# Prompt-type pooling rewritten as one recurrence per chunk, with its weights computed on 32 segments

## Chip, cores and metric

The kernel runs on one core of one Trainium2 chip. The metric is the device time of one execution in microseconds (us): the median of three runs of the kernel before is 1771.83 us (1770.89 to 1772.97). Engines are named as the profile names them: PE is TensorE (matmul), PEld its weight load, DVE is VectorE, ACT is ScalarE, POOL is GpSimd, SP is SyncE. POOL, SP and ACT also issue DMAs[...].

## What is computed

Sixteen images `x` of 512 positions by 512 features, all in fp32.

```python
# stage 1: a two-layer MLP whose last 128 outputs come from one of 16 experts, chosen per image
h = gelu(x @ fc1_w.T + fc1_b)                       # 512 -> 2048
shared = h @ fc2_w.T + fc2_b                        # 2048 -> 384
expert = h @ experts_w[idx].T + experts_b[idx]      # 2048 -> 128
x1 = x + concat(shared, expert)
# stage 2: attention pooling with one score per position; the mask depends on the prompt type
scores = tanh(x1 @ W1 + b1) @ v                     # one number per position l
mask = prefix (l <= j) if type 0, postfix (l >= j) if type 1, l != j if type 2
p = softmax(where(mask, scores[l], -1e30))          # over l, for each j
out = x1 + (p @ x1) / count(mask)
```

Since the score does not depend on j, row j of `p @ x1` is a running sum: a prefix of exponentials times x1 for type 0, a suffix for type 1, the whole without one element for type 2. A recurrence along the positions, rescaled whenever the running maximum grows, computes it.

## The kernel before, in words

Features lie on the partitions (four chunks of 128), positions along the free axis, so `x1T` of one image is 128 x 4 x 512. The program is written out by hand (`manual_schedule`, line 60): what each engine does, and in which order, is the order of the code. The image loop stands at line 493; image b's MLP is interleaved with the pooling of image b-1.

**fc1** (`fc1_group`, line 240) works in four groups of 256 + 256 hidden rows. Each group is a two-by-two block product done with seven block products instead of eight, in the order ba, bb, bc, bd, ba, bc, bd, named by the PSUM bank they write. The operands are sums of blocks: those of the weights are computed once, for image 0, on DVE (`sums`, line 69; four 128x512 sums per group), written to DRAM and read back for later images (`fetch`, line 85); those of x are four sums on DVE (`x_sums`, line 115). Between the products DVE joins results: u2 (line 260), u3 (264), c22 (268), c21 (276), c12 (281); ACT copies bank ba once (256) and applies gelu (250). A bank is written again once its readers are through: the second product into bc waits for u3, the second into bd for c22, the first product of the next group, into ba, for the gelu of ba. In group 1 of each image (group 2 of image 0) DVE also makes four 128x1024 sums of the expert's weights (`lower`, line 172), one in each of four slots.

**fc2** (`fc2`, line 285) is the same scheme with 16 matmuls to a half product. Its operand sums are four 128x2048 DVE instructions (313 to 321). The residual x arrives by DMA again (`residual`).

**Pooling of the image before** is a generator whose steps are handed out by `slot()` after each fc1 product (line 507) and by `at()` between the fc2 products (line 520). `scores` (347) makes the projection `pa`, tanh, and a score product whose stationary operand is v copied to 128 columns, so that every partition holds the whole score row. `recur` (362) then works on 128 partitions x 512 positions for all prompt types at once: a forward and a backward running maximum (scans), their exponentials on ACT (three passes, each between two table loads), three weights e for the part before, the own position and the part behind, the denominators, one reciprocal. Then for each of the four chunks nine DVE instructions (439 to 455): two products, a forward and a backward scan, three products and two sums. `flip` (459) transposes a finished chunk back on PE, ACT copies it to SBUF, POOL writes it to DRAM. In the image loop (line 523) 37 steps of the recurrence are spread over fc2. After the last image the whole pooling of image 15 stands alone (542 to 546).

**The start.** The x blocks of image 0 are loaded over ACT's queue and the first weights over SP's. Seven small inputs (idx, prompt types, biases, w1, v) go over POOL's queue behind the four stores of the first weight sums (139 to 151). DVE's order there is: x sums, four weight sums, `rows` from idx (159), the copy of v (186), masks and counts (193 to 212), then the sums of group 1 and u2. `load_fc2` puts two transfers of 2 MB and 1 MB on SP's queue ahead of the weights of group 2.

Of the kernel before, what the change touches and what calls it, by code (L numbers as in the profile page):

```python
# [17 lines left out]
def tile_cond_experts_then_prompt_pool(  # L18
# [26 lines left out]


# [38 lines left out]
    def fetch(b, g):  # L85
# [11 lines left out]
        for n, t in (("a11", w["a11"]), ("a21", a21), ("a22", w["a22"]), ("a12", w["a12"])):  # L97
            nc.sync.dma_start(t, part_of(n))
# [26 lines left out]
    x_next = load_x(0, nc.scalar)  # L125
    fc1b_sb = const.tile([P, NH], F32, name="fc1b_sb")
    nc.scalar.dma_start(fc1b_sb, fc1_b)
    xs_next = x_sums(0, x_next)
    w_next = fetch(0, 0)
    work(4)  # L130
    fc2_sb = const.tile([P, NH, 2 * P], F32, name="fc2_sb")
# [5 lines left out]

    idx_sb = const.tile([P, B], I32, name="idx_sb")
    nc.gpsimd.dma_start(idx_sb, idx.partition_broadcast(P))
    pt_sb = const.tile([P, B], I32, name="pt_sb")  # L140
    nc.gpsimd.dma_start(pt_sb, ptype.partition_broadcast(P))
    fc2b_sb = const.tile([P, NS], F32, name="fc2b_sb")
    nc.gpsimd.dma_start(fc2b_sb, fc2_b)
    expb_sb = const.tile([E, PART], F32, name="expb_sb")
    nc.gpsimd.dma_start(expb_sb, exp_b)
    w1_sb = const.tile([P, ND, A], F32, name="w1_sb")
    nc.gpsimd.dma_start(w1_sb, w1)
    b1_sb = const.tile([A, 1], F32, name="b1_sb")
    nc.gpsimd.dma_start(b1_sb, b1)
    v_sb = const.tile([A, 1], F32, name="v_sb")  # L150
    nc.gpsimd.dma_start(v_sb, v)
# [7 lines left out]
    nc.vector.tensor_scalar(rows, idx_sb, float(P), part_f, ALU.mult, ALU.add)  # L159

# [17 lines left out]
    ex_next = load_expert(0)  # L178

# [5 lines left out]
    v_bc = const.tile([A, P], F32, name="v_bc")  # L185
    nc.vector.tensor_copy(v_bc, v_sb.to_broadcast([A, P]))


    cnt_i = p1.tile([P, 2, S], I32, tag="ff", name="cnt_i")
    nc.gpsimd.iota(cnt_i[:, 0, :], pattern=[[1, S]], base=1, channel_multiplier=0)  # L190
    nc.gpsimd.iota(cnt_i[:, 1, :], pattern=[[-1, S]], base=S, channel_multiplier=0)
    cnts = const.tile([P, 2, S], F32, name="cnts")
    nc.vector.tensor_copy(cnts, cnt_i)


    is0 = const.tile([P, B], F32, name="is0")
    nc.vector.tensor_scalar(is0, pt_sb, 0.0, None, ALU.is_equal)
    is1 = const.tile([P, B], F32, name="is1")
    nc.vector.tensor_scalar(is1, pt_sb, 1.0, None, ALU.is_equal)
    is2 = const.tile([P, B], F32, name="is2")  # L200
    nc.vector.tensor_scalar(is2, pt_sb, 2.0, None, ALU.is_equal)

    pen = const.tile([P, 3, B], F32, name="pen")
    for i, sel in enumerate((is1, is2, is0)):
        nc.vector.tensor_scalar(pen[:, i, :], sel, NEG, None, ALU.mult)

    cnt2 = const.tile([P, B], F32, name="cnt2")
    nc.vector.tensor_scalar(cnt2, is2, float(S - 1), None, ALU.mult)
# [138 lines left out]
    def scores(b, x1T):  # L347
        pa = ps_l.tile([A, S], F32, tag="l", name=f"pa_{b}")
        for dc in range(ND):
            nc.tensor.matmul(  # L350
                pa, w1_sb[:, dc, :], x1T[:, dc, :], start=(dc == 0), stop=(dc == ND - 1)
            )
        aT = p1.tile([A, S], F32, tag="aT", name=f"aT_{b}")
        nc.scalar.activation(aT, pa, AF.Tanh, bias=b1_sb)
        yield
        psc = ps_l.tile([P, S], F32, tag="l", name=f"psc_{b}")
        nc.tensor.matmul(psc, v_bc, aT, start=True, stop=True)
        sc = p1.tile([P, S], F32, tag="sc", name=f"sc_{b}")
        nc.scalar.copy(sc, psc)
        yield sc  # L360

    def recur(b, x1T, sc, ready):
        V = nc.vector

        def rev(t):
            return t[..., S - 1 :: -1]

        def border(tag, name, at, value):
            t = p1.tile([P, S + 1], F32, tag=tag, name=f"{name}_{b}")
            nc.gpsimd.memset(t[:, at : at + 1], value)  # L370
            return t

        mf, mb = border("mf", "mf", 0, NEG), border("mb", "mb", S, NEG)
        V.tensor_tensor_scan(mf[:, 1:], sc, sc, NEG, ALU.max, ALU.max)
        yield
        ff = p1.tile([P, 2, S], F32, tag="ff", name=f"ff_{b}")
        V.tensor_tensor(ff[:, 0, :], mf[:, :S], mf[:, 1:], ALU.subtract)
        yield  # L380
        V.tensor_tensor(ff[:, 1, :], sc, mf[:, 1:], ALU.subtract)
        yield
        V.tensor_tensor_scan(rev(mb), rev(sc), rev(sc), NEG, ALU.max, ALU.max)
        nc.scalar.activation(ff, ff, AF.Exp)
        yield
        fb = p1.tile([P, 2, S], F32, tag="fb", name=f"fb_{b}")
        V.tensor_tensor(fb[:, 0, :], mb[:, 1:], mb[:, :S], ALU.subtract)
        yield
        V.tensor_tensor(fb[:, 1, :], sc, mb[:, :S], ALU.subtract)
        yield  # L390

        t = p1.tile([P, S], F32, tag="t", name=f"t_{b}")
        mx = p1.tile([P, S], F32, tag="mx", name=f"mx_{b}")
        V.tensor_scalar(t, mf[:, :S], pen[:, 0, b : b + 1], None, ALU.add)
        nc.scalar.activation(fb, fb, AF.Exp)
        yield
        V.scalar_tensor_tensor(mx, sc, pen[:, 1, b : b + 1], t, ALU.add, ALU.max)
        yield
        V.scalar_tensor_tensor(mx, mb[:, 1:], pen[:, 2, b : b + 1], mx, ALU.add, ALU.max)
        yield  # L400
        e = p1.tile([P, 3, S], F32, tag="e", name=f"e_{b}")
        for i, src in enumerate((mf[:, :S], sc, mb[:, 1:])):
            V.scalar_tensor_tensor(e[:, i, :], src, pen[:, i, b : b + 1], mx, ALU.add, ALU.subtract)
            yield
        zf, zb = border("mf", "zf", 0, 0.0), border("mb", "zb", S, 0.0)
        V.tensor_tensor_scan(zf[:, 1:], ff[:, 0, :], ff[:, 1, :], 0.0, ALU.mult, ALU.add)
        nc.scalar.activation(e, e, AF.Exp)
        yield
        V.tensor_tensor_scan(rev(zb), rev(fb[:, 0, :]), rev(fb[:, 1, :]), 0.0, ALU.mult, ALU.add)
        yield  # L410
        cnt = p1.tile([P, S], F32, tag="mx", name=f"cnt_{b}")
        V.tensor_scalar(cnt, cnts[:, 0, :], is0[:, b : b + 1], cnt2[:, b : b + 1], ALU.mult, ALU.add)
        yield
        V.scalar_tensor_tensor(cnt, cnts[:, 1, :], is1[:, b : b + 1], cnt, ALU.mult, ALU.add)
        yield

        den = p1.tile([P, S], F32, tag="sc", name=f"den_{b}")
        tb = p1.tile([P, S], F32, tag="t", name=f"tb_{b}")
        V.tensor_tensor(den, e[:, 0, :], zf[:, :S], ALU.mult)
        yield  # L420
        V.tensor_tensor(tb, e[:, 2, :], zb[:, 1:], ALU.mult)
        yield
        V.tensor_tensor(den, den, e[:, 1, :], ALU.add)
        yield
        V.tensor_tensor(den, den, tb, ALU.add)
        yield
        V.tensor_tensor(den, den, cnt, ALU.mult)
        yield
        V.reciprocal(den, den)
        yield  # L430
        for i in range(3):
            V.tensor_tensor(e[:, i, :], e[:, i, :], den, ALU.mult)
            yield
        for dc in range(ND):
            x1 = x1T[:, dc, :]
            f, h = border("xf", f"xf{dc}", 0, 0.0), border("xb", f"xb{dc}", S, 0.0)
            wf = p1.tile([P, S], F32, tag="wf", name=f"wf_{b}_{dc}")
            wb = p1.tile([P, S], F32, tag="wb", name=f"wb_{b}_{dc}")
            V.tensor_tensor(wf, x1, ff[:, 1, :], ALU.mult)  # L439
            yield  # L440
            V.tensor_tensor_scan(f[:, 1:], ff[:, 0, :], wf, 0.0, ALU.mult, ALU.add)  # L441
            yield
            V.tensor_tensor(wb, x1, fb[:, 1, :], ALU.mult)
            yield
            V.tensor_tensor_scan(rev(h), rev(fb[:, 0, :]), rev(wb), 0.0, ALU.mult, ALU.add)  # L445
            yield
            V.tensor_tensor(wf, f[:, :S], e[:, 0, :], ALU.mult)
            yield
            V.tensor_tensor(wb, h[:, 1:], e[:, 2, :], ALU.mult)  # L449
            yield  # L450
            V.tensor_tensor(wf, wf, wb, ALU.add)  # L451
            yield
            V.scalar_tensor_tensor(x1, e[:, 1, :], 1.0, x1, ALU.add, ALU.mult)  # L453
            yield
            V.tensor_tensor(x1, x1, wf, ALU.add)  # L455
            ready.append(dc)
            yield
# [9 lines left out]
    class Pooling:  # L467
# [8 lines left out]
        def score(self):  # L476
            sc = next(self.first)
            if sc is not None:
                self.rest = recur(self.b, self.x1T, sc, self.ready)
# [109 lines left out]
```

## Time and profile before

| | us |
|---|---|
| median of three runs | 1771.83 |
| the profiled execution, its own time | 1772.12 |
| its span, first to last instruction | 1770.3 |
| PE busy / DVE busy / ACT busy | 1662.6 / 1322.5 / 544.0 |
| one image in the middle (105 us window): PE, DVE, ACT busy | 102.73, 80.94, 34.24 |
| DVE SCAN 128x512, mean of one | 1.22 |
| DVE TENSOR_TENSOR 128x512 / 128x1024 / 128x2048 | 0.68 / 1.21 / 2.28 |
| ACT Exp 128x1024, gelu 128x256 | 1.06, 0.50 |
| POOL DMA of 256 KB to DRAM, issue to landing | 2.7 |
| expert row of 1 MB by indirect DMA | 5.7 |

A PE product of eight fp32 128x256 matmuls is one row in the order of time; the starts of two rows give its true length (1.73 us), since the ends overlap. A wait line reads: engine, what waited, its line, what it waited for, its line, then total time, number and longest. In a group line "idle before" is the time that the engine stood still ahead of these instructions, with what ended it.

### The profile page before, as it was taken

To read this page: it belongs to the slowest core of one execution; us is meant where nothing else is said; L and a number is where in the kernel's file an instruction comes from. 1 tells how busy PE (TensorE), PEld (TensorE's weight loads), DVE (VectorE), ACT (ScalarE), POOL (GpSimd) and SP (SyncE) were. 2 spreads that over 40 slices of the span, in tenths; PEclk is the share of its full clock that TensorE was granted. 3 is DMA by queue.
4 is the path that set the end of the run, shared out by engine and by line. 5 is a ranking of instruction groups with operands and counts; after the bars stand their busy time and mean duration, and the time that the engine had idled before them with its cause. 6 is when DMAs were issued, how large, how long until landed. Compare 5 with 4: busy or idle time off the path is not lost.

```text
span 1770.3 us, 20281 instructions
## 1 busy us (share of the span) xinstructions
PE 1662.6 (94%) x7586; PEld 1420.3 (80%) x7586; DVE 1322.5 (75%) x1665; ACT 544.0 (31%) x941; POOL 95.0 (5%) x304
## 2 busy tenths in 40 slices
PE   5999999999999999999999999999999999999960
PEld 4888888788888878888887888878888887888850
DVE  2628959597695958959597795959869596895968
ACT  1305142150513406052251523316051240514210
POOL 2000000001000000000001000000000001000000
PEclk8999999999999999999999999999999999999985
DMA  7424342333524233342433423233342433433000
GB/s 242 154 86 126 102 125 78 125 96 101 161 77 126 89 117 116 101 136 67 137 89 118 140 95 118 81 123 108 101 144 66 140 99 107 131 101 119 19 18 24
DMA packets 136035, 190.39 MB, mean 108 GB/s; under 512 B 10897, under 2 KB 97985, under 8 KB 133889
## 3 DMA queue, kind: packets, MB, share of 16 engines
q1 hardware_dynamic: 125728, 149.98, 28.1%
q0 software_dynamic: 8976, 38.04, 6.5%
q8 instruction: 61, 1.00, 0.2%
q10 hardware_dynamic: 1232, 1.06, 0.2%
q14 instruction: 38, 0.30, 0.1%
HBM read 168.07 MB, written 20.97 MB: 107 GB/s over the span
## 4 chain that ended last, share of the span: by engine, by line
PE 63%; DVE 29%; issue 7%; DMA 1%; ACT 0%; POOL 0%; POOLq 0%; DVEq 0%; ACTq 0%
PE bc L224 18%; PE ba L224 17%; PE bd L224 16%; PE bb L224 7%; DVE xb L445 3%; DVE xf L441 3%; PE pa L350 3%; DVE wb L449 2%; DVE t L313 2%; DVE wf L451 2%; DVE hT L321 2%; DVE hT L318 2%; DVE x1T L455 2%; DVE wf L439 2%; DVE x1T L453 2%
## 5 line engine op out<-in xcount | busy, mean ns | idle before, releaser
L224 PE MATMUL ba<-xT,w_a 128*128 128x256 f32 x1024 | 243.8, 381 | 4.6 <-DMA xT<-in_xT 4.6
L224 PEld LDWEIGHTS ba<-xT,w_a 128*128 128x128 f32 x1024 | 195.6, 191 | 31.3 <-DMA xT<-in_xT 4.6
L250 ACT ACTIVATE hT<-c,fc1b_sb 128x256 f32<-128x256 f32 x384 | 172.4, 501 | 106.7 <-DVE c L276 58.1
L302 ACT ACTIVATE xr<-xr,fc2b_sb 128x256 f32<-128x256 f32 x96 | 43.3, 498 | 361.0 <-DMA xr<-in_xT 338.1
L224 PE MATMUL bc<-xs,w_a 128*128 128x256 f32 x512 | 122.8, 383 | 11.3 <-DVE u L264 11.3
L260 DVE TENSOR_TENSOR u<-bb,p1s 128x512 f32<-128x512 f32 x64 | 44.1, 689 | 111.8 <-PE bb L224 107.3
L224 PE MATMUL bb<-xs,w_s 128*128 128x256 f32 x512 | 122.8, 383 | 4.4 <-DVE w_s L74 4.4
L224 PEld LDWEIGHTS bc<-xs,w_a 128*128 128x128 f32 x512 | 98.3, 192 | 31.6 <-DVE u L264 11.7
L224 PE MATMUL bd<-xT,w_s 128*128 128x256 f32 x512 | 121.2, 379 | 0.0
L224 PE MATMUL bc<-xs,w_s 128*128 128x256 f32 x512 | 121.1, 379 | 0.0
L250 ACT ACTIVATE hT<-ba,fc1b_sb 128x256 f32<-128x256 f32 x128 | 53.8, 471 | 218.7 <-PE ba L224 217.6
L224 PE MATMUL bd<-xs,w_s 128*128 128x256 f32 x512 | 121.0, 379 | 0.0
L224 PEld LDWEIGHTS bb<-xs,w_s 128*128 128x128 f32 x512 | 98.3, 192 | 25.1 <-issue 7.2
L462 PE MATMUL py<-ident,x1T 128*128 128x128 f32 x256 | 42.0, 289 | 81.0 <-DVE x1T L455 81.0
L224 PE MATMUL bd<-hT,fc_lo 128*128 128x256 f32 x512 | 115.8, 379 | 0.0
L224 PE MATMUL bd<-hT,exp 128*128 128x256 f32 x512 | 115.7, 379 | 0.0
L224 PE MATMUL ba<-hT,fc_sb 128*128 128x256 f32 x512 | 113.2, 379 | 0.0
L224 PE MATMUL bb<-hT,fc_sb 128*128 128x256 f32 x512 | 113.1, 379 | 0.0
L256 ACT COPY p1s<-ba 128x512 f32<-128x512 f32 x64 | 37.1, 580 | 240.0 <-PE ba L224 235.6
L462 PEld LDWEIGHTS py<-ident,x1T 128*128 128x128 f32 x256 | 29.2, 146 | 99.1 <-issue 85.1
L224 PEld LDWEIGHTS bd<-xT,w_s 128*128 128x128 f32 x512 | 97.6, 191 | 13.4
L224 PEld LDWEIGHTS bc<-xs,w_s 128*128 128x128 f32 x512 | 97.6, 191 | 13.4
(136 smaller groups left out, 2944.4 us busy)
## 6 DMA issues: line engine op xcount, KB each, us to landing
w_s<-w1s_s SPq DMA_DIRECT2D x240, 256.0 KB, 2.7
w_a<-in_fc1T SPq DMA_DIRECT2D x192, 256.0 KB, 2.9
xr<-in_xT SPq DMA_DIRECT2D x64, 256.0 KB, 3.1
out_y<-yo POOLq DMA_DIRECT2D x64, 256.0 KB, 2.7
xT<-in_xT SPq DMA_DIRECT2D x60, 256.0 KB, 4.6
w1s_s<-w_s POOLq DMA_DIRECT2D x16, 256.0 KB, 4.2
fc_sb<-in_fc2T SPq DMA_DIRECT2D x1, 2048.0 KB, 20.7
xT<-in_xT ACTq DMA_DIRECT2D x4, 256.0 KB, 6.6
```

The lines of the kernel that those rows point to most:

```text
L224: nc.tensor.matmul(bank[:, m, :], w(m, k), mv[:, k, :], start=(not add and m == 0 and k == 0), stop=(k == depth - 1), skip_group_check=True,)
L250: nc.scalar.activation(hT[:, hc, ts(c, HC)], src[:, m, :], AF.Gelu, bias=fc1b_sb[:, hc : hc + 1])
L256: nc.scalar.copy(p1s, ba)
L260: nc.vector.tensor_tensor(u2, bb, p1s, ALU.add)
L302: nc.scalar.activation(t[:, m, :], t[:, m, :], AF.Identity, bias=bias)
L313: add(t1, b12, b11, ALU.subtract)
L318: add(b11, b22, t1, ALU.subtract)
L321: add(b21, b21, b11, ALU.subtract)
L350: nc.tensor.matmul(pa, w1_sb[:, dc, :], x1T[:, dc, :], start=(dc == 0), stop=(dc == ND - 1))
L441: V.tensor_tensor_scan(f[:, 1:], ff[:, 0, :], wf, 0.0, ALU.mult, ALU.add)
L445: V.tensor_tensor_scan(rev(h), rev(fb[:, 0, :]), rev(wb), 0.0, ALU.mult, ALU.add)
L462: nc.tensor.transpose(py[:, jt, :], x1T[:, dc, ts(jt, P)], ident)
```

## The change

The score product has v itself as stationary operand, so the scores land in one row on one partition. ACT copies this row twice, forward and reversed, and two DMAs lay each copy out as 32 segments of 16 positions on 32 partitions. The prompt type picks one of the two: type 1 is computed as type 0 on the reversed row. 41 small DVE instructions on 32 partitions (21 ahead of one Exp, 20 behind it) compute three coefficient rows c1, beta, c0 and three scalars. Segments are joined by 32x32 transposes and scans over one row. Type 2 uses whole sums, with the position of the maximum (`max`, `max_index`) set apart and mended at the end. The coefficients are written to DRAM by two DMAs and read back, broadcast to 128 partitions, by a third; ACT adds reversed copies of two of them.

Then each chunk takes four wide DVE instructions and three ACT instructions: u = x1 * c1; ACT reverses u into the other half of its tile and accumulates its sum; one scan over the half that the prompt type selects (a register offset, loaded by DVE from DRAM); ACT scales and offsets the result and reverses it; product with beta; sum into x1. Budgets and pauses in `slot` say in which fc1 slots the pieces lie: scores in slots 1 and 3 of an image, weights from slot 6, a pause of two slots behind the Exp and of five behind the broadcast DMA, then the chunks. What is left is finished at the start of fc2. The transposes go by blocks of 128 positions, all behind the last chunk, and the writes to DRAM are contiguous. The many constants of `recur` go; new ones are filled in one step of group 1 of image 0.

At the start x goes over SP's queue, the first weights over ACT's behind idx, and the other small inputs follow on ACT's queue.

By the built program's instruction order, in one image the weights' first part (lines 423 to 453 of the changed kernel) stands around c12 of group 0, the second behind the first expert sum of group 1, the third and fourth behind the third and fourth; the apply steps begin behind u3 of group 2. On ACT the turning copy of the coefficients stands behind the first copy of bank ba in group 2, and six apply instructions (chunks 0 and 1) stand between it and the gelu of ba.

```diff
-    x_next = load_x(0, nc.scalar)
...
-    w_next = fetch(0, 0)
...
+    nc.scalar.dma_start(idx_sb, idx.partition_broadcast(P))
+    x_next = load_x(0)
+    w_next = fetch(0, 0, nc.scalar)
...
+    fc1b_sb = small("fc1b", [P, NH], fc1_b)
+    pt_sb = small("pt", [P, B], ptype.partition_broadcast(P), I32)
...
+        def score(self):
+            b = self.b
+            psc = ps_l.tile([1, S], F32, tag="l", name=f"psc_{b}")
+            nc.tensor.matmul(psc, v_sb, self.aT, start=True, stop=True)
...
+            nc.scalar.copy(self.srow[:, 0, :], psc)
+            nc.scalar.copy(self.srow[:, 1, :], psc[:, S - 1 :: -1])
...
+                self.queue.dma_start(self.s2[:, k, :], self.srow[:, k, :])
...
+        def weights(self):
...
+            V.tensor_scalar(s, self.s2[:, 0, :], col(not1), None, ALU.mult)
+            V.scalar_tensor_tensor(s, self.s2[:, 1, :], col(is1), s, ALU.mult, ALU.add)
...
+            V.tensor_tensor_scan(ml[:, SL - 1 :: -1], s, s, NEG, ALU.max, ALU.max)
...
+            V.transpose(mt, ml)
...
+            V.max(m8, self.srow[:, 0, :])
...
+            V.max_index(i8, m8, self.srow[:, 0, :])
...
+            nc.scalar.activation(ex[:, 32 : 65 + SL], ex[:, 32 : 65 + SL], AF.Exp)
...
+            yield -2
...
+            V.tensor_tensor_scan(zl, f0, g1, 0.0, ALU.mult, ALU.add)
...
+            V.reciprocal(z, z)
...
+            self.queue.dma_start(row[: 3 * S].rearrange("(k p c) -> p k c", k=3, c=SL), co)
+            self.queue.dma_start(row[3 * S : 3 * S + 3].unsqueeze(0), sc[0:1, :3])
+            cb = self.cb = p1.tile([P, ROW + 2 * S], F32, tag="cb", name=f"cb_{b}")
+            self.queue.dma_start(cb[:, 2 * S : ROW + 2 * S - 1], row[: ROW - 1].partition_broadcast(P))
+            yield -5
+
+            nc.scalar.copy(
+                cb[:, : 2 * S].rearrange("p (k s) -> p k s", k=2),
+                cb[:, 2 * S : 4 * S].rearrange("p (k s) -> p k s", k=2)[:, :, S - 1 :: -1],
+            )
+            yield -1
+
+        def apply(self):
...
+            turn = V.snap(V.value_load(ptype[b : b + 1].unsqueeze(0), min_val=0, max_val=2) % 2)
...
+            jm = V.value_load(self.jmax[0:1, 0:1], min_val=0, max_val=S - 1)
...
+            def offset(dc):
+                V.tensor_scalar(U[:, dc : dc + 1], T[:, dc : dc + 1], kap, xm[:, dc : dc + 1], ALU.mult, ALU.add)
+                v[dc] = p1.tile([P, 2 * S], F32, tag="v", name=f"v_{b}_{dc}", bufs=2)
+                nc.scalar.activation(v[dc][:, :S], f[dc], AF.Identity, bias=U[:, dc : dc + 1], scale=fac)
+                nc.scalar.copy(v[dc][:, S:], v[dc][:, S - 1 :: -1])
...
+            for dc in range(ND + 2):
+                if dc < ND:
+                    u = p1.tile([P, 2 * S], F32, tag="u", name=f"u_{b}_{dc}", bufs=2)
+                    V.tensor_tensor(u[:, :S], x1T[:, dc, :], c1, ALU.mult)
+                    nc.scalar.activation(u[:, S:], u[:, S - 1 :: -1], AF.Identity, accum_out=T[:, dc : dc + 1])
+                    yield 0.6
+                if dc >= 2:
+                    V.tensor_tensor(f[dc - 2], turned(v[dc - 2]), beta, ALU.mult)
+                    yield 0.6
+                    V.tensor_tensor(x1T[:, dc - 2, :], x1T[:, dc - 2, :], f[dc - 2], ALU.add)
+                    yield 0.6
+                if dc < ND:
+                    f[dc] = p1.tile([P, S], F32, tag="f", name=f"f_{b}_{dc}", bufs=3)
+                    V.tensor_tensor_scan(f[dc], c0, turned(u), 0.0, ALU.mult, ALU.add)
+                    offset(dc)
+                    yield 1.2
+            V.scalar_tensor_tensor(at_max, T, gam, at_max, ALU.mult, ALU.add)
...
-            def slot(n=[0], g=g):
+            def slot(n=[7 * g]):
                 n[0] += 1
                 work(1)
                 if pool:
-                    if (g, n[0]) in ((0, 1), (0, 5)):
+                    if n[0] == 1:
+                        pool.project()
+                    elif n[0] == 3:
                         pool.score()
-                    if g:
-                        pool.run(1 + (n[0] in (1, 5)))
+                    elif n[0] > 5:
+                        pool.slot(1.0)
...
         def at(name):
...
-                pool.run({"1": 6, "2": 10, "5": 9, "7": 9, "6": 3}.get(name, 0))
-                if name in "576":
-                    pool.flips(1 if name != "6" else 0)
+                while name == "1" and not pool.done:
+                    pool.slot(1e9)
+                if name in "257":
+                    for t in {"2": (0,), "5": (1, 2), "7": (3,)}[name]:
+                        pool.flip(t)
```

## The prediction

> **What bounds the kernel now.** I read the core list first: one core, full clock, so no throttling has to be explained.
>
> ```profile
> core 0: 1770.3 us, clock 0.982
> ```
>
> Then the busy shares and the chain that ended last.
>
> ```profile
> PE 1662.6 (94%) x7586; PEld 1420.3 (80%) x7586; DVE 1322.5 (75%) x1665; ACT 544.0 (31%) x941; POOL 95.0 (5%) x304
> ...
> PE 63%; DVE 29%; issue 7%; DMA 1%; ACT 0%; POOL 0%; POOLq 0%; DVEq 0%; ACTq 0%
> ```
>
> PE is the bound. DVE's 29% of the chain is not 29% of prize; what can be won is PE's idle time. By stages:
>
> ```profile
> 25.00:50.00 25.00, 16.92 (x69) 14.59 (x70) 12.11 (x27) 5.05 (x12) 6.44 (x13) 0.80 0.82 276
> ...
> 115.00:1690.00 1575.00, 1540.95 (x7069) 1318.93 (x7068) 1214.08 (x1516) 512.26 (x884) 74.16 (x253) 1.00 0.35 107
> 1690.00:1770.00 80.00, 26.92 (x111) 19.96 (x109) 56.01 (x74) 9.63 (x13) 5.32 (x18) 0.67 0.07 20
> ```
>
> Fifteen images of 105 us lie in the middle window, and PE is idle 34 us in all of it. The waits on PE say where:
>
> ```profile
> PE py L462 <- DVE x1T L455: 81.0, 34, 29.0
> PE bc L224 <- DVE u L264: 11.3, 1, 11.3
> ```
>
> Some 47 of the 81 us are in the tail (29.0 and three of 6.0), the rest two short waits per image; the 11.3 is in the head. The order of time on PE shows one image:
>
> ```profile
> 831.94 0.66 PE L462 MATMUL py<-ident,x1T 128*128 128x128 f32 x4 [0.60 <-DVE x1T L455]
> ...
> 835.89 3.62 PE L224 MATMUL bd<-hT,exp 128*128 128x256 f32 x16
> 841.17 0.63 PE L462 MATMUL py<-ident,x1T 128*128 128x128 f32 x4 [1.66 <-DVE x1T L455]
> ...
> 862.98 1.89 PE L224 MATMUL ba<-xT,w_a 128*128 128x256 f32 x8
> ...
> 889.72 1.89 PE L224 MATMUL bd<-xT,w_s 128*128 128x256 f32 x8
> ...
> 968.59 1.89 PE L224 MATMUL ba<-xT,w_a 128*128 128x256 f32 x8
> ```
>
> The period is 968.59 - 862.98 = 105.6 us. fc1 runs without a gap, a product each 1.73 us; in fc2 the gaps before the transposes are 0.75 + 1.83 + 0.15 = 2.7 us (starts, less the normal 3.45 or 0.46 us). That is all the middle can give: 15 x 2.7 = 41 us. fc1 has little slack: the last product of a group waits until VectorE has emptied bank bd (c22):
>
> ```profile
> 888.44 0.66 DVE L268 TENSOR_TENSOR c<-bd,u 128x512 f32<-128x512 f32 x1
> 889.02 1.21 DVE L74 TENSOR_TENSOR exs<-fc_sb,exs 128x1024 f32<-128x1024 f32 x1
> ```
>
> Bank bd is free at 889.1 and PE wants it at 889.72.
>
> [...]
>
> **The body, part by part.** Time 0 is an image's first product (862.98). Without waits fc1 ends at 52.64 (915.62).
>
> *Removed:* 51 wide VectorE instructions for the weights and per-chunk steps (some 49 us an image) and three Exp passes. This empties fc2 of pooling: I count all 2.7 us as gained, since the transposes then wait for work finished long before.
>
> *The weights on 32 partitions:* 41 VectorE instructions. A TENSOR_SCALAR of 16 elements took 0.17 us with starts 0.08 apart; one that waits for its predecessor I put at 0.20; max and its index at 0.69 each, like 512 elements. Sum 7.9 us (6.5 to 10). By the built order they begin after group 0's c21 (15.5), and to the last of them lie also c12, u2, u3, c22 (0.60 each) and the four expert sums (1.13 each): 6.9 us. VectorE never idles there, so the last coefficient is ready at 15.5 + 14.8 = 30.2. On the way c22 of group 1 ends at 27.35 where PE wants the bank at 26.75: a first wait of 0.65 us.
>
> *The round trip through DRAM:* three transfers on POOL. The second write follows the last coefficient[...], then the broadcast of 770 KB: between 2.7 and 5.7, by size 4.7. Landed at 30.3 + 2.2 + 4.7 = 37.2 (33.5 to 41). ScalarE then turns 1024 columns: 1.06 (the Exp row of that size). The first multiply starts at S = 38.3. Its earliest is 34.8, behind u3 of group 2. The pause of slots puts this copy in ScalarE's queue at 32, so it and all behind it stand still: p1s and gelus queue up.
>
> *The two register loads (three reads):* [...]4 at the worst; hidden while they end before S, bare if the broadcast is early.
>
> *The apply steps* alternate between engines: multiply (VectorE) -> reverse (ScalarE) -> scan -> scale (ScalarE) -> reverse (ScalarE) -> multiply. The scan reads half of u at a register offset, so it waits for the reversal. Behind them wait c22, c21, c12 on VectorE and the gelu of bank ba on ScalarE, so PE's banks. From S, with multiply 0.69, scan 1.23, gelu pair 0.84 by their rows[...]: multiply ends 0.70, reverse 1.5, scan 2.8, c22 3.4: the last product of group 2 starts at S+3.5. Chunk 1: scale and copy of chunk 0 to 4.3, reverse 5.0, scan 6.3, scale and copy 7.9, and only then gelu of ba, 8.6: group 3 starts at S+8.65. Further down: reverse of chunk 2 at 10.1 (behind gelus), scan 11.4, scale, copy, gelu, reverse of chunk 3 to 14.5, scan 15.7, u2, two wide steps, u3 18.3, two more, c22 20.2. Group 3's last product runs S+20.3 to S+22.0. With S = 38.3 fc1 ends at 60.3 instead of 52.64: 7.65 us lost. The waits are 0.65, 2.3, 3.4, 1.1 and 0.2.
>
> Net per image 7.65 - 2.7 = +4.95; fifteen images: +74 us.
>
> **Head.** idx comes first, so VectorE no longer stands behind v_sb (wait of 4.9) and idx (4.8), and PE's 11.3 us goes. Next late: group 2's weights. SP is held by the fc2 transfers until 28.84 and issued a21 at 40.45, behind a tile; now it can at 35.4, 5 us earlier; the sums of group 2 follow. I take -6 (0 to -12). Seven small transfers on ScalarE's queue, 0.5 us each, stand ahead of its first copy, which PE's first product covers until 8.4; uncovered they cost 1 to 2 us.
>
> **Tail.** Scores at 1713.4 as before; two row copies 1.2, load 2.2, weights 7.9 with Exp 0.3, round trip 6.9, turn 1.1: 1733. Apply with nothing between: four chunks of the chain, 16.5: 1749.5. The last row took 6.8 us from x1T to the end; four transposes in a row add 2.2: 1758.5 against 1770.3: -12 (-6 to -18).
>
> **Sum** against the profiled execution: 1772.1 (span 1770.3 and 1.8 around it) - 6 - 12 + 74 = 1828. The median of the runs is 1771.8, so nothing is corrected.
>
> **Rivals.** (1) *VectorE's relief wins.* 15 x 2.7 + 18 = 59: 1713 if fc1 keeps up. For it: VectorE does 27 us less per image. Against: the loss S - 30.65 must fall under 3.9 for any gain, S under 34.5, before u3 lets the first multiply start. It needs data landed by 33.5 and a chain some 2 us shorter or more; I centre it at 1745. (2) *Data early, chain as worked out:* S = 34.8, loss 4.15, net +1.45: 1772 - 18 + 22 = 1776. (3) *Slow broadcast,* 128 readers of one row, or bare register loads, or a PE clock that falls in waits of 3 us (after 4.4 us in the head a product took 3.78 instead of 1.89): S = 41.5 gives +123: 1877. That the change would not do what it says is not in question: the built order holds all of it.
>
> **Chances.** My forecast (1781 to 1872) 0.70, (1) 0.14, (2) 0.06, (3) 0.10. Under 0.2% (3.5 us) this kernel's runs can't tell from no change: faster 0.14, same 0.04, slower 0.82. The range runs from 1765, which takes in (2), to 1880; it leaves out most of (1) and the end of (3), about 0.18.
>
> **What would show it.** Period near 110.6; waits per image of PE on gelu of ba (3.4 us), on c22 (2.3), on u3 (1.1), none on the transposes; ScalarE waiting some 5 us on the broadcast at its turning copy; tail from the last x1T to the end near 50 us. I am wrong if the broadcast lands by 33.5, or if the scan does not wait for ScalarE, or if the waits on PE in fc1 stay under 2.7 us.

## The result, and the profile after

| | before | after |
|---|---|---|
| median of the runs, us | 1772.17 (4 runs) | 1883.05 (4 runs, 1879.39 to 1885.36) |
| span of the profiled execution | 1770.3 | 1877.5 |
| PE's stalls in one image of the body, by the starts of its rows, us | 2.7, in fc2 | 9.4, in fc1 |
| DVE busy | 1322.5 | 917.8 |

The change makes the kernel slower: the ratio is 1.0624, 95% interval 1.0604 to 1.0645. It lies beyond the end of the forecast range (1880). The changed kernel's busy shares:

```profile
PE 1706.5 (91%) x7586; PEld 1434.3 (76%) x7586; DVE 917.8 (49%) x1718; ACT 563.5 (30%) x1137; POOL 101.6 (5%) x179
```

VectorE has 405 us less to do, and the profiled execution takes 107 us more (the medians differ by 111). The stages (time, PE, PE load, DVE, ACT, POOL busy, granted clock, DMA share) say where:

```profile
115.00:1690.00 1575.00, 1471.22 (x6568) 1236.55 (x6567) 784.04 (x1465) 490.67 (x993) 82.27 (x139) 0.98 0.35 110
```

In this window PE is idle 104 us instead of 34, and 7069 matmuls became 6568. Where PE waits (total us, times, longest):

```profile
PE bd L232 <- DVE c L276: 74.3, 30, 5.3
PE py L575 <- DVE x1T L570: 35.6, 1, 35.6
PE ba L232 <- ACT hT L258: 28.8, 15, 3.2
PE bc L232 <- DVE u L272: 13.9, 9, 7.5
```

The transposes wait once, in the tail. In their place stand two waits per image on bank bd, which c22 has to empty, and one on bank ba, which a gelu has to empty. One image in the order of time on PE, whose first product is at 915.18:

```profile
940.48 1.89 PE L232 MATMUL bc<-xs,w_a 128*128 128x256 f32 x8
943.73 1.99 PE L232 MATMUL bd<-xT,w_s 128*128 128x256 f32 x8 [1.36 <-DVE c L276]
...
954.19 1.89 PE L232 MATMUL bc<-xs,w_a 128*128 128x256 f32 x8
959.35 3.41 PE L232 MATMUL bd<-xT,w_s 128*128 128x256 f32 x8 [3.27 <-DVE c L276]
964.54 1.99 PE L232 MATMUL ba<-xT,w_a 128*128 128x256 f32 x8 [1.78 <-ACT hT L258]
...
974.23 1.99 PE L232 MATMUL bc<-xs,w_a 128*128 128x256 f32 x8 [0.79 <-DVE u L272]
...
977.99 7.07 PE L232 MATMUL ba<-hT,fc_sb 128*128 128x256 f32 x32
```

By the starts, against 1.73 us per product, the four stalls cost 1.52, 3.43, 3.46 and 0.95 us; fc2 starts 62.81 us after the first product instead of 52.64. The 0.8 us that the four stalls leave out are 0.1 to 0.2 us behind stalls, where the rows restart slower, and 0.3 around the new score product (fc1 without a stall takes 52.93 us in experiments 9 and 10). VectorE in the same image, from u3 of group 2 to the first multiply:

```profile
950.94 0.69 DVE L272 TENSOR_TENSOR u<-bc,u 128x512 f32<-128x512 f32 x1 [0.72 <-PE bc L232]
955.43 0.23 DVE L539 TENSOR_SCALAR xm<-x1T,is 128x4 f32 x1 [3.80 <-issue]
955.83 0.69 DVE L557 TENSOR_TENSOR u<-x1T,cb 128x512 f32<-128x512 f32 x1 [0.18 <-issue]
```

The gap ahead of xm (3.80 us, "issue") is the register loads: VectorE waits for nothing that the order of time shows. The loads themselves stand under their source lines as instructions of VectorE's queue (shortest, median and longest in ns): the address of the prompt type, its value, and the position of the maximum, which lies in SBUF.

```profile
L532 DVEq TENSOR_LOAD <-in_ptype_ptr x16: 1418/2293/2735, 156.9 to 1841.8; - x16
L532 DVEq TENSOR_LOAD <-in_ptype x16: 508/518/995, 159.2 to 1843.3; - x16
L536 DVEq TENSOR_LOAD <-i x16: 545/550/558, 160.1 to 1844.2; - x16
```

The address takes most of the time. ScalarE's turning copy had ended at 954.94, 0.9 us before the multiply. The multiply starts at 955.83, so S = 40.65; over the fifteen images S lies between 40.28 and 42.68, mean 41.00. VectorE's waits show both late arrivals side by side:

```profile
DVE xm L539 <- issue: 60.3, 16, 4.4
...
DVE u L557 <- ACT cb L523: 8.0, 5, 3.1
```

Of sixteen poolings, eleven have the register loads as the last to end by these lines, five the copy of the broadcast data (in one of the five the gap is 0.18 us, as behind the loads, so that it may belong with the eleven).

Counted by the projection pa, which starts each image's pooling: the head up to the first pa takes 122.83 us (125.45 before), an image 113.56 (105.61, both the mean of the fourteen distances between image starts), the tail from the last pa to the end 53.1 (62.4). With fifteen images that is -2.6 + 119 - 9.4 = 107 us.

### The profile page after: what moved, and what is told of

Read it like the earlier page. It is cut to its first block, busy times and chain, and to the rows that moved or that the text cites. A ratio compares the mean times of both kernels' runs of the same rounds, so it can differ in the third digit from the quotient of the medians.

```text
span 1877.5 us, 20914 instructions
## 1 busy us (share of the span) xinstructions
PE 1706.5 (91%) x7586; PEld 1434.3 (76%) x7586; DVE 917.8 (49%) x1718; ACT 563.5 (30%) x1137; POOL 101.6 (5%) x179
## 5 line engine op out<-in xcount | busy, mean ns | idle before, releaser
L232 PE MATMUL ba<-xT,w_a 128*128 128x256 f32 x1024 | 256.9, 396 | 36.1 <-ACT hT L258 28.8
L232 PEld LDWEIGHTS ba<-xT,w_a 128*128 128x128 f32 x1024 | 201.9, 199 | 73.4 <-ACT hT L258 37.3
L232 PE MATMUL bd<-xT,w_s 128*128 128x256 f32 x512 | 145.1, 433 | 74.3 <-DVE c L276 74.3
L232 PEld LDWEIGHTS bd<-xT,w_s 128*128 128x128 f32 x512 | 107.1, 216 | 105.2 <-DVE c L276 89.0
L232 PEld LDWEIGHTS bd<-xs,w_s 128*128 128x128 f32 x512 | 96.0, 190 | 25.4 <-PE bc L232 13.0
L232 PEld LDWEIGHTS bb<-hT,fc_sb 128*128 128x128 f32 x512 | 97.3, 190 | 13.2
L232 PEld LDWEIGHTS bd<-hT,exp 128*128 128x128 f32 x512 | 97.3, 190 | 13.2
L232 PEld LDWEIGHTS ba<-hT,fc_sb 128*128 128x128 f32 x512 | 97.2, 190 | 13.2
L232 PEld LDWEIGHTS bd<-hT,fc_lo 128*128 128x128 f32 x512 | 96.1, 190 | 12.4
```

Of the source, the lines that this page charges most:

```text
L232: nc.tensor.matmul(bank[:, m, :], w(m, k), mv[:, k, :], start=(not add and m == 0 and k == 0), stop=(k == depth - 1), skip_group_check=True,)
```

## The experiments

The theory from these profiles: fc1 ends 22 us after S whatever decides S, since everything behind the first multiply stands in order in the queues of VectorE and ScalarE; and S is decided by two things that end within 1 us of each other, the register loads and the broadcast with its copy. Rivals: the register loads alone, the broadcast alone, or the small weight instructions and what lies between them. S in this section is the mean over the fifteen images of the body, by VectorE's order of time in the one profiled execution of each kernel.

**1. Register loads earlier** (`loads_early`): behind c12 of group 1, in front of u2 of group 2.

```diff
-            yield -5
+            yield -3
+            self.turn = V.snap(V.value_load(ptype[b : b + 1].unsqueeze(0), min_val=0, max_val=2) % 2)
+            self.jm = V.value_load(self.jmax[0:1, 0:1], min_val=0, max_val=S - 1)
+            yield -2
```

> The register loads of each image stand behind the last coefficient and c12 of group 1, before u2 of group 2, instead of behind u3. Main theory (two late arrivals side by side: the register loads, which end some 40.3 us after the image's first product, and the broadcast with its turning copy, which ends at 39.7 to 40 in most images): the copy becomes the last, the first multiply S moves from 40.65 to about 39.9, and 15 x 0.8 = 12 us are won: about 1871 (1860 to 1878). Rival, the loads alone decide: S falls to just behind u3, 37, and the time to about 1830. Rival, the broadcast alone decides: 1883, no change.

Measured: 1873.51 us (1.057 of the kernel before, 1.0552 to 1.0587), S = 40.64. VectorE in one image:

```profile
949.23 0.22 DVE L542 TENSOR_SCALAR xm<-x1T,is 128x4 f32 x1
953.26 0.69 DVE L560 TENSOR_TENSOR u<-x1T,cb 128x512 f32<-128x512 f32 x1 [3.81 <-ACT cb L526]
```

The gap has not gone, its name has changed: "issue" became a wait for ScalarE's copy. With the loads alone as cause this had to give 1830, so that rival is out. With the broadcast alone it had to give nothing: the 10 us by the medians (6 by the periods) are near that, and what rules it out is experiment 2.

**2. Data early** (`early_data`): the broadcast reads a constant row, right behind the scores.

```diff
+            cb = self.cb = p1.tile([P, ROW + 2 * S], F32, tag="cb", name=f"cb_{b}")
+            self.queue.dma_start(cb[:, 2 * S : ROW + 2 * S - 1], fc1T[0, 0, : ROW - 1].partition_broadcast(P))
...
-            self.queue.dma_start(cb[:, 2 * S : ROW + 2 * S - 1], row[: ROW - 1].partition_broadcast(P))
```

> The broadcast of every image reads a constant row of the inputs and is issued right behind the scores, so nothing waits for coefficients; the two writes of coefficients stay, unread. The output is not the reference's: the pooling is applied with coefficients that mean nothing. Main theory (two late arrivals): the loads still start behind u3 and end at 40.3, so S moves by only 0.3 to 0.5 us in the body, some 6 us, and about 3 in the tail: 1874 (1866 to 1881). Rival, the broadcast alone decides: S falls to some 36.8 and the time to about 1820.

Measured: 1858.76 us (1.0487, 1.047 to 1.0505), S = 39.73. More was won than expected, because the loads themselves became shorter:

```profile
941.91 0.69 DVE L272 TENSOR_TENSOR u<-bc,u 128x512 f32<-128x512 f32 x1 [0.71 <-PE bc L232]
945.57 0.23 DVE L540 TENSOR_SCALAR xm<-x1T,is 128x4 f32 x1 [2.96 <-issue]
```

2.96 us without the broadcast under way, against 3.80 beside it (means over the body 2.84 and 3.80). It is the load of the address that shrinks, from 2.29 to 1.55 us in the median. The two causes are not only parallel, one lengthens the other. Still, with the data long there, S is far from the 36.8 of the rival.

**3. The prompt type from SBUF** (`loads_sbuf`), so that the loads of the address and of the value from DRAM become one load from SBUF.

```diff
-            turn = V.snap(V.value_load(ptype[b : b + 1].unsqueeze(0), min_val=0, max_val=2) % 2)
+            turn = V.snap(V.value_load(pt_sb[0:1, b : b + 1], min_val=0, max_val=2) % 2)
```

> The prompt type is read into its register from its copy in SBUF; in the changed kernel it is read from DRAM, by two loads (an address, then the value), and the register loads took 3.8 to 4.4 us beside the broadcast, 2.7 to 2.9 us in the kernels where the broadcast was not under way. Theory: the read from DRAM is the slow one, and the broadcast slows it; then VectorE's stretch without an instruction ahead of xm falls from 3.8 us to under 2 us, and the turning copy is last in nearly all images (S near 40.2 to 40.4, time near 1873, as with the loads moved). Rival: each load costs the same wherever it reads; then the stretch stays at about 2.5 to 3.8 us, and the time is within 5 us of 1883 or just below.

Measured: 1876.0 us in one run, S = 40.52.

```profile
949.99 0.69 DVE L272 TENSOR_TENSOR u<-bc,u 128x512 f32<-128x512 f32 x1 [0.72 <-PE bc L232]
951.48 0.23 DVE L539 TENSOR_SCALAR xm<-x1T,is 128x4 f32 x1 [0.80 <-DVE u L272]
954.12 0.69 DVE L557 TENSOR_TENSOR u<-x1T,cb 128x512 f32<-128x512 f32 x1 [2.41 <-ACT cb L523]
```

The gap ahead of xm is 0.80 instead of 3.80 us: the read from DRAM is the slow one, and the two loads from SBUF take 0.31 and 0.32 us. The time hardly moves, because the copy takes its place, as in experiment 1. S fell by 0.48 us, but the period only by 0.13: more of the products in fc1 ran at half clock here than in the changed kernel (below experiment 6).

**4. Both late arrivals away** (`both_sbuf`): the edits of 2 and 3 together.

> Constant row for the broadcast, issued early (the pooling then has coefficients that mean nothing), and the prompt type read from SBUF: both late arrivals of the changed kernel taken away at once. Theory of two late arrivals side by side: 24 us were won by the first alone, some 7 to 10 by the second alone; with both the first multiply stands 1.2 us behind u3 of group 2, S = 37.6 instead of 40.9, and the period is S + 72.5 = 110.1: 15 x 3.3 = 50, and 3 in the tail: about 1829. If the two act independently: 1883 - 24 - 7 = 1852.

Measured: 1828.86 us in one run, S = 37.75. The first multiply now stands right behind u3 and the loads:

```profile
930.60 0.69 DVE L272 TENSOR_TENSOR u<-bc,u 128x512 f32<-128x512 f32 x1 [0.72 <-PE bc L232]
932.10 0.23 DVE L540 TENSOR_SCALAR xm<-x1T,is 128x4 f32 x1 [0.81 <-DVE u L272]
932.50 0.69 DVE L558 TENSOR_TENSOR u<-x1T,cb 128x512 f32<-128x512 f32 x1 [0.17 <-issue]
```

Experiment 2 won 24 us and experiment 3 won 7, a single run; together they win 54. In the periods it is 1.04, 0.13 and 3.01 us an image. That is what two late arrivals side by side must show; independent costs would have added up to 31 us, or 1.2 an image.

**5. Expert sums out of the weights' way** (`exs_fc2`): in group 1 they stood between the small instructions.

```diff
-            if g == (1 if b else 2):
+            if g == 2 and not b:
...
+            if name == "1":
+                work(4)
...
+        if b:
+            exw = lower(p1, ex_raw, 1, "exs")
```

> The four expert sums (1.13 us each) stand at the beginning of fc2 instead of between the small weight instructions in group 1. The last coefficient is then ready some 3 us earlier and the wait of 1.36 us on c22 of group 1 is gone. Main theory: the broadcast is early, but the register loads behind u3 decide; u3 itself comes 1.36 us earlier, so S moves by 1.4 and the time by 15 x 1.4 = 20: about 1861 (1852 to 1872). Rival, the lag of the small instructions with the broadcast behind them is the whole loss: S follows by 3.5 to 4, about 1826.

Measured: 1839.41 us (1.0377, 1.036 to 1.0395), S = 38.10, right between the two cases. The last coefficient is ready at 27.3 instead of 31.5, the copy ends at 37.0 in the mean, and the loads again decide S:

```profile
930.99 0.69 DVE L272 TENSOR_TENSOR u<-bc,u 128x512 f32<-128x512 f32 x1 [0.98 <-PE bc L232]
934.45 0.23 DVE L539 TENSOR_SCALAR xm<-x1T,is 128x4 f32 x1 [2.76 <-issue]
934.85 0.69 DVE L557 TENSOR_TENSOR u<-x1T,cb 128x512 f32<-128x512 f32 x1 [0.17 <-issue]
```

u3 comes 1.7 us earlier in the image (34.1 instead of 35.8), since the stall on c22 of group 1 is gone, and the loads take 1.0 us less, since the broadcast now lands early in them. My expectation had the first of these two and lacked the second, which experiment 2 explains.

**6. Expert sums and loads** (`exs_loads`): the edits of 1 and 5.

> Both: expert sums at the beginning of fc2 and register loads before u2 of group 2. Main theory: now neither is late; the broadcast lands near 35.8, its copy ends near 36.9, S is about 37.0 instead of 40.65, and fc1 ends at S + 22: 15 x 3.65 = 55 us won, about 1828 (1815 to 1842), far more than the sum of either part alone (12 + 20). Rival, the two parts act independently of each other: 1851. The period should be near 109.9.

Measured: 1821.60 us (1.0286, 1.0269 to 1.0303), S = 36.93, period 109.51: the main theory's 1828 within its range. The rival's 1851 took 20 us for experiment 5, which won 44; with the measured 10 and 44, independent parts would give 1830, so this run says little against independence, and experiments 2 to 4 carry that point. PE's waits in this version:

```profile
PE ba L232 <- ACT hT L258: 46.2, 15, 3.2
PE py L578 <- DVE x1T L573: 35.4, 1, 35.4
PE bd L232 <- DVE c L276: 17.7, 15, 2.5
```

One wait on bd per image instead of two; the wait on gelu stays. This version leaves nothing out and has both late arrivals moved forward, and it is still slower than the kernel before: the chain of 22 us in fc1 alone costs more than fc2 gave.

All seven kernels with the apply steps in fc1 lie on one line. Period is the mean distance of the image starts (the last image, which loads no successor, left out):

| kernel | S | period | period - S |
|---|---|---|---|
| changed kernel | 41.00 | 113.56 | 72.56 |
| loads_early | 40.64 | 113.16 | 72.52 |
| loads_sbuf | 40.52 | 113.43 | 72.91 |
| early_data | 39.73 | 112.52 | 72.79 |
| exs_fc2 | 38.10 | 110.88 | 72.78 |
| both_sbuf | 37.75 | 110.55 | 72.80 |
| exs_loads | 36.93 | 109.51 | 72.58 |

S varies by 4.1 us, the difference by 0.4. What moves S moves the period by the same amount, but for that 0.4. Most of it is PE's clock. In experiments 4 and 6 eight images of thirty have no stretch at half clock (a granted clock of 0.5), and in all eight fc1 ends 22.16 us behind S; in all but one of the other 22 it ends 22.37 to 23.81 us behind. The means are 22.46 in the changed kernel and 22.79 in loads_sbuf, which has the largest difference.

**7. Weights only** (`weights_only`): turning copy, loads and apply steps left out.

```diff
         def run_all(self):
             yield from self.weights()
-            yield from self.apply()
+            return
+            yield
```

> The weights, their writes and the broadcast stay; the turning copy, the register loads and the apply steps are left out, so the output is the residual result without the pooling. Theory: all that the weights cost PE is the wait of 1.36 us on c22 of group 1, and fc2 has lost its 2.7 us of gaps: period 105.6 - 2.7 + 1.4 = 104.3, and the tail is some 25 us shorter than 53. About 1713. If the broadcast or the small instructions cost more by themselves, the period is above 105.

Measured: 1717.09 us in one run, period 104.68, fc2 starting at 54.56. So the weights with their three transfers cost 54.56 - 52.64 = 1.9 us an image (1.6 at c22 of group 1, 0.3 around the score product), fc2 has lost its gaps (50.1 us from its start to the next image), and all else in the changed kernel's period, 113.56 - 104.68 = 8.9 us an image, is the apply steps where they stand, with their copy and loads.

**8. Apply steps in fc2** (`apply_fc2`): the same instructions behind the second product of fc2, all sixteen transposes behind the fifth.

```diff
-            yield -5
+            yield -99
...
-                while name == "1" and not pool.done:
+                while name == "2" and not pool.done:
...
-                if name in "257":
-                    for t in {"2": (0,), "5": (1, 2), "7": (3,)}[name]:
+                if name == "6":
+                    for t in range(NT):
```

> All apply steps with the turning copy and the register loads stand behind the second product of fc2 instead of in groups 2 and 3 of fc1, and the sixteen transposes ahead of the first writes into x1T. Theory: the loss in fc1 is only that steps of an alternating chain of 17 to 22 us stand in the queues in front of c22, u2, u3 and the gelu of ba, each wanted within a product (1.73 us); in fc2 a product is 6.9 us and VectorE and ScalarE have some 30 us with nothing to do. Only the 1.36 us on c22 of group 1 stay: period 104.1 to 104.5, time 1738 (1730 to 1752). Rival: the chain costs PE wherever it stands (the transposes then wait, as before the change, or the sums of fc2 do); 1765 to 1800.

Measured: 1760.02 us, 0.9926 of the kernel before (0.991 to 0.9943). The same steps, moved and not shortened, win 123 us against the changed kernel. Less than I expected, though: 1760 lies between the range of the theory (to 1752) and that of the rival (from 1765), and the period is 105.7. The transposes, in a row, wait for ScalarE to empty their bank:

```profile
947.11 3.62 PE L232 MATMUL ba<-hT,exs 128*128 128x256 f32 x16
950.57 1.04 PE L575 MATMUL py<-ident,x1T 128*128 128x128 f32 x8
952.27 1.14 PE L575 MATMUL py<-ident,x1T 128*128 128x128 f32 x8 [0.67 <-ACT yo L577]
```

fc2 takes 51.1 us instead of 50.1, and fc1 54.56, not the 54.0 that I had reckoned (52.64 and the wait of 1.36): 1.2 to 1.6 us an image over what was expected. What is won lies in head and tail; the body is as long as before.

**9. Apply steps in fc2, expert sums in group 3** (`apply_fc2_exs`). The expectation says groups 2 and 3; in the trace all four sums stand in group 3.

```diff
-            if g == (1 if b else 2):
+            if g == (3 if b else 2):
```

> As the one before, and the four expert sums in groups 2 and 3, where VectorE now has time, instead of between the small weight instructions. The last wait in fc1 goes: period 102.9, 15 x 1.36 = 20 us less than the one before, 1718 (1710 to 1732). Rival: the sums then delay u2, u3 or c22 of groups 2 and 3 by up to 1 us each: within 5 us of the one before.

Measured: 1734.33 us (0.9783, 0.9767 to 0.98), period 103.99. The step from 8 to 9 is 25.7 us, 1.7 per image, which prices the expert sums between the weights: the wait on c22 of group 1 is gone from PE's waits. The level is 16 us above what was expected, just outside the range, mostly by the 1.0 us an image of the transposes again.

**10. The version that the runs point to** (`best`): 9, with the prompt type from SBUF and the transposes in two pairs.

```diff
-        add(out_block(0, 0), bb, p1x, ALU.add)
-        add(out_block(1, 1), ba, p57, ALU.add)
         product(bc, of("s4"), b22, KH, add=True)
         at("3")
+        add(out_block(0, 0), bb, p1x, ALU.add)
+        add(out_block(1, 1), ba, p57, ALU.add)
...
+                if name in "63":
+                    for t in {"6": (0, 1), "3": (2, 3)}[name]:
```

> Apply steps in fc2, expert sums in groups 2 and 3, the prompt type read from SBUF, and the transposes two by two, ahead of the seventh and behind the eighth of fc2's halves, with the two first writes into x1T moved behind them. Theory: the 0.67 us that PE waited for ScalarE's copy between four transposes in a row goes, fc1 takes 52.9 and fc2 50.1: period 103.0 against 103.86, 13 us less than the version with the sums moved: 1721 (1715 to 1728), 0.971 of the kernel before. Rival: the moved writes delay the next image's first product or the scores, then 1734 or above.

Measured: 1720.52 us, 0.9703 of the kernel before (0.969 to 0.9717), period 103.0.

```profile
115.00:1655.00 1540.00, 1540.00 (x7083) 1319.67 (x7082) 848.76 (x1569) 527.94 (x1063) 87.72 (x148) 1.00 0.36 117
```

PE is busy for all of the body. Its waits on other engines and on DMAs in this kernel lie in head and tail (0.8 us on the tanh is not shown):

```profile
PE py L575 <- DVE x1T L570: 35.3, 1, 35.3
PE bc L232 <- DVE u L272: 8.9, 1, 8.9
PE ba L232 <- DMA w_a<-in_fc1T: 7.5, 1, 7.5
PE bb L232 <- DVE w_s L77: 1.9, 1, 1.9
```

## Why the prediction was wrong

*Direction and mechanism held.* Slower was given 0.82. fc1 was said to end at S + 22.0: over fifteen images it ended at S + 22.46 (63.46 - 41.00): at S + 22.16 or a hundredth less in eight of them, later in the others by products at half clock. The two wide stalls in the shown image were forecast as 2.3 and 3.4 and cost 3.43 and 3.46, the one on u3 1.1 and 0.95. The waits on the transposes went as said, and fc2 with them became 50.1 us long; the whole 2.7 us was gained.

*The step that failed is S: 38.3 forecast, 41.00 measured.* It is a sum of the weights and the round trip through DRAM, with the register loads beside it, and each term was undersized:
- "The last coefficient is ready at 15.5 + 14.8 = 30.2": it is ready at 31.5. The weights begin 0.25 us later (15.75), and the 41 small instructions take 8.9 us from start to start, not 7.9; the wide ones between take the 6.9 that I had. Where one small instruction reads the result of the one before, the starts are 0.19 to 0.32 us apart, where I had put 0.20. (A single TENSOR_TENSOR of 16 elements took 0.15 to 0.17 us.) The same term makes the stall on c22 of group 1 1.52 us, not 0.65.
- The round trip: in experiment 1, where only the data decides, S stands 40.64 - 31.51 = 9.1 us behind the last coefficient; I had 8.1. The 2.2 us in it for the write were an estimate of mine that no row of the kernel before showed; in the changed kernel the two writes landed after 2.3 and 1.9 us in the median. Half of the difference is the write: the broadcast is issued 2.8 us behind the last coefficient in the mean, not 2.3, since POOL is still issuing the first write (0.56 us) and the second leaves 0.3 us late. The other half is the broadcast, which I sized right by its median in the changed kernel (4.7 us) but which takes 4.3 to 6.8 by image there, and 5.2 in the mean in experiment 1.
- "Hidden while they end before S": the register loads begin only behind u3 of group 2 and were not hidden: 3.8 us ahead of xm, near the 4 that I had called the worst (an estimate of mine: the kernel before has no register load). With the broadcast also late, they cost only 41.00 - 40.64 = 0.36 in this kernel; without it they would hold S at 39.7 by themselves (experiment 2). In the changed kernel the value took 0.52 us in the median and the load from SBUF 0.55; the address alone took 1.11 in experiment 8, 1.55 in experiment 2, and 2.29 beside the broadcast.

1.3 + 1.0 + 0.4 = 2.7 us. The chain adds 0.46 (0.16 of its own, 0.30 by the half clock), and fc2 is 0.15 shorter than forecast: 3.0 an image, 15 x 3.0 = 45 of the 51 us by which the sum missed. The rest is at the ends.

*Head:* -2.6 against -6. PE no longer waits 11.3 us for u3 of group 0. It waits 7.5 for u3 of group 1 instead, behind the sums of group 2, so the "next late" that I named took more of it; and its first product starts at 7.37 instead of 4.56, since the first weights arrive later over ScalarE's queue. The start of the first pa also differs by 2.6 us (121.4 to 124.0) among these kernels, whose heads are the same, so this term carries no more than its sign.

*Tail:* -9.4 against -12. The first multiply (24.0 us behind the last pa, 25.1 forecast) and the apply chain (16.8 us, 16.5 forecast) were right within 1.1 us. ScalarE's terms in that chain were estimates of mine that no row of the kernel before showed; in the changed kernel the reversal took 0.62 us and its sum 0.19, the scaling 0.81 and the copy 0.62. Behind the chain I had not counted that the output tiles are two, so that the third copy waits for the store of the first. ScalarE in the tail:

```profile
1867.39 0.59 ACT L577 COPY yo<-py 128x512 f32<-128x512 f32 x1 [0.27 <-PE py L575]
1869.82 0.59 ACT L577 COPY yo<-py 128x512 f32<-128x512 f32 x1 [1.85 <-DMA out_y<-yo]
```

*The range.* Rival (3), a slow broadcast or bare register loads with S = 41.5 and 1877 us, is nearly what happened. All three causes that it names came, each in part, the PE clock that falls in waits with 0.3 us an image. I gave it 0.10 and cut the range at 1880. My bounds (small instructions up to 10 us, landing up to 41, loads up to 4) each held the measured mean. I took the middle of each and treated the upper ends as one rare case. But the small instructions and the round trip lie in series, so their errors add, and the later of data and loads decides in each image; where the terms are all estimates of something that no row shows, the sum's upper end is not rare.

*What the runs prove and what they don't.* That S sets the period is shown by seven kernels; that two late arrivals decide S, by experiments 1 to 4; that the place of the steps and not their amount is the loss, by experiments 7, 8 and 10. In experiment 10 two things changed at once and were not tried apart; the 1.0 us an image that it wins over experiment 9 is all in fc2 (50.1 instead of 51.1), whose transposes no longer wait. That PE's clock makes most of the scatter among the seven is read from the traces, and so is the split of the round trip. That the head's small gain goes into the weights of group 2 is read from the trace and was not tried.

## What to carry to other kernels

Taking work from an engine that is at 75% gains only what the bound engine was waiting for (here 2.7 us an image and the tail), and new small steps are paid by what they stand in front of. A chain that alternates between two engines belongs where both have slack as long as the chain: in fc1 a bank is wanted back every 1.73 us, in fc2 every 6.9, and the same chain cost 9 us an image in one place and nothing in the other, once the transposes were out of its way (fc2 takes 50.1 us in experiment 10 as in experiment 7, which has no chain). When two things arrive late side by side, removing one shows little; remove both before you call either harmless.

## What the hardware showed that I had not expected

- VectorE's register loads took longer with a value in DRAM than with both in SBUF, and longest beside the broadcast: the gap ahead of xm was 0.80 us with both values in SBUF, 2.8 to 3.0 with the prompt type in DRAM, and 3.8 (up to 4.4) beside the 770 KB broadcast. The load of the address is what grows: 1.55 us in the median in experiment 2, 2.29 in the changed kernel; the value took 0.52.
- PE's clock after a wait: at the end of the wait of 3.27 us in the changed kernel the granted clock was 0.5 for 3.41 us, and the product behind it took 3.41 us instead of 1.89. In that image it cost nothing, since the next product waited for a gelu anyway; in others it did. In experiment 6 fourteen waits took 3.19 us: behind ten of them the next product started 2.8 to 3.6 us after the first, behind four 1.83. The fifteen half-clock stretches in the body of the changed kernel begin on one grid of 3.413 us and last 3.41, 6.83 or 10.24. What sets the ten waits apart from the four was not shown.
- ScalarE's reversal with a sum took 0.62 us and then 0.19 more for reading out the accumulator, which stands in the profile as an instruction of its own.
